# The first layer of a two-layer graph network as seven products of quadrants with 129-column halves, the second norm's operand in one buffer, and the residual in the second step

## The chip, the cores and the metric

The kernel runs on one core of one Trainium2 chip. The metric is device time in microseconds (us) of one execution of the program; the median of three runs before the change is 2427.76 us (2426.85 to 2429.27). Below, PE is the matrix engine (TensorE) and PEld its loading of the stationary operand, DVE is VectorE, ACT is ScalarE, POOL is GpSimd and SP is SyncE, which issues the DMAs. L137 is line 137 of the kernel, where every matmul is recorded; L35 is the helper that records nearly every operation of the other engines, so that these are told apart by their tiles.

## The reference

Two layers of graph attention over x of shape (64, 256, 512) in float32, with one 256x256 adjacency matrix for the whole batch. Each layer takes a layer norm and a relu of x and adds its output to x.

```python
# layer 0
h = jnp.maximum(_layernorm(x), 0.0)
H = jnp.einsum('bnf,fo->bno', h, W)              # 512 -> 256
e = H @ a[0] + swapaxes(H @ a[1], 1, 2)          # 256 x 256 per batch
e = leaky_relu(e, 0.2) - 1e9 * (1 - adj)
out = softmax(e, -1) @ H
x = x + concatenate([out, H], -1)
# layer 1: 8 heads of 64
h = jnp.maximum(_layernorm(x), 0.0)
q, k, v = (split_heads(h @ W.T + b) for each of q, k, v)
attn = softmax(where(adj == 0, -inf, q @ k.T / 8), -1)
x = x + merge_heads(attn @ v) @ Wo.T + bo
```

## The kernel before, in words

The 64 batches are taken in 32 groups `g` of two batches `b` (512 tokens, four row tiles of 128). There is no hardware loop: everything is unrolled, and generators that stand for stages are advanced by hand. Group `g` is in its attention (`scores`, `mask_pairs`, `fold`, `weigh`, `outputs`) while group `g+1` is in `project` (q, k, v), group `g+2` in `first_layer` and group `g+3` in `first_norm`. One period is one group; it has two steps, b = 0 and b = 1, each with a string (`steps`) of letters that says in which order the stages advance: S the scores, m masking of a pair of heads, n a piece of the first norm, s a piece of `first_layer`, u a product of `project`, o a product of `outputs`, f a piece of `fold` (the row sums of the attention), r half of `residual`, v `value_differences`. The step (g=0, b=0) has a string of its own. At the start of a step, `weigh` emits the products p·v of the step before (tile `pr`), and the scores (`sc`) follow.

What fixes the order on each engine: all matmuls and transposes of PE are pinned in the order in which they are written (`in_order`). On the other engines `not_sooner` pins an operation behind the one written last on its engine; operations without it are placed by the tile framework's scheduler. SP's DMA issues are pinned as well, and a DMA waits in SP's queue until its data is there.

PSUM: matmul results take one of five banks in turn (`mm`, tag `turn`), so that a product can start only when the bank that was used five allocations ago has been read; three more banks are held for `project` and `outputs`. The pr banks of a step are read by DVE into `oT0` and `oT1` (with `r`, the reciprocals of the row sums); the scores take eight banks, `sc_0` to `sc_7`, two in alternation, and `sc_3` comes round to the bank that `oT0` frees.

The first norm: DVE takes the statistics of `x`, POOL a power and a factor of them (`factor`), ACT normalizes into `xn` (two buffers), DVE transposes 32x32 blocks into `xt`, a DMA writes them out (`passed`), four DMAs fetch them (`moved`), and ACT copies them with a relu into the operand: `hT0` for the first layer, one 128x4x256 tile for each batch, and `hT1` for the second, one 128x4x512 tile for each group.

The first layer: 258 columns, which are two score columns (`W` times the two vectors of `a`) and behind them the 256 of `W`. For each of four row tiles, four matmuls of 128 rows by 258 columns over 512 features add up in one bank `ph`, ACT copies it into `H`, and POOL adds H to the right half of x. Then `rows` (a DVE transpose of the score columns), a DMA through DRAM to `own`, four ACT additions into `e`, leaky relu of `e` on DVE (`scalar_tensor_tensor`, twice, both inputs in SBUF), exp on ACT, masking on DVE and the products `po`.

The projections q, k and v and the outputs are done already as seven products of quadrants instead of eight (a scheme of Winograd's: `operand_sums` makes s1 = a21+a22, s2 = s1−a11, s3 = a11−a21 and s4 = a12−s2, and overwrites a21 with s3; `weight_sums` does the like for the weights; `seven` says which operand meets which weight). Their results are assembled with a product kept in SBUF (tag `kept`, three buffers) and one or two products that add up in a bank.

The residual: `residual(g+1)` adds the rows `b_out` of the output bias to x of group g+1, four POOL operations of 128x512. It is written in the first step of each period.

Of the kernel before, what the change touches and what calls it, by code (L numbers as in the profile page):

```python
# [57 lines left out]
def bounded(  # L58
# [50 lines left out]
    def mm(name):  # L109
        return psum.tile([P, 512], F32, tag="turn", name=name, bufs=5)  # L110
# [25 lines left out]
    def matmul(*args, **kwargs):  # L136
        in_order(nc.tensor.matmul(*args, **kwargs))  # L137
# [28 lines left out]

    w0_sb = const.tile([P, HP, F1 + 2], F32, name="w0_sb")
    nc.sync.dma_start(w0_sb[:, :, 2:], w0.rearrange("(c p) o -> p c o", p=P))
    adj_i = att.tile([P, NT, N], I32, tag="kept", name="adj_i", bufs=3)
    nc.sync.dma_start(adj_i, adj.rearrange("(t p) k -> p t k", p=P))  # L170

# [79 lines left out]
    square_ones = big.tile([P, P], F32, tag="o_sums", name="square_ones", bufs=1)  # L251
    gpsimd.memset(square_ones, 1.0)

    def weight_sums(name):
        w = w_sb[name]
        not_sooner(vector, "tensor_sub", w[:, :, T3, :], w[:, :, W22, :], w[:, :, W12, :])
        vector.tensor_sub(w[:, :, T1, :], w[:, :, W12, :], w[:, :, W11, :])
        vector.tensor_sub(w[:, :, T2, :], w[:, :, W22, :], w[:, :, T1, :])
        vector.tensor_sub(w[:, :, T4, :], w[:, :, W21, :], w[:, :, T2, :])

    def last_bias():

# [230 lines left out]

    def operand_sums(engine, quads, sums):
        a11, a12, a21, a22 = quads
        not_sooner(engine, "tensor_add", sums[:, 0], a21, a22)
        engine.tensor_sub(sums[:, 1], sums[:, 0], a11)

        not_sooner(engine, "tensor_sub", a21, a11, a21)
        engine.tensor_sub(sums[:, 2], a12, sums[:, 1])  # L500

    def seven(quads, sums):

        a11, a12, s3, a22 = quads
        s1, s2, s4 = (sums[:, i] for i in range(3))
        return {
            1: (a11, W11), 2: (a12, W21), 3: (s4, W22), 4: (a22, T4),  # L510
            5: (s1, T1), 6: (s2, T2), 7: (s3, T3),
        }
# [5 lines left out]
    def first_norm(g):  # L518

        xt = {}  # L520
        mv = small.tile([P, GT, 2], F32, tag="mv", name=f"mv0_{g}", bufs=4)
        factors, norm, turn, fetch, put = norm_T(xt, mv, f"0_{g}", g == 0)
        for b in range(GB):
            for t in range(NT):
                xt[b * NT + t] = xs[g, b][:, t, :]
                stats(mv, xt, b * NT + t, f"0_{g}")
            factors(b)
            yield
            norm(b)
            yield  # L530
            turn(b)
            if g == 1:
                fetch(b)
            yield
            if g <= 1:

                other = g == 0 and b == 1
                pool, tag, bufs = (att, "moved", 2) if other else (big, "hT0", 1)
                hT0[g, b] = pool.tile([P, HP, N], F32, tag=tag, name=f"hT0_{g}_{b}", bufs=bufs)
                put(b, hT0[g, b])  # L540
                if g == 1:
                    yield
        if g <= 1:
            return
        for b in range(GB):
            fetch(b, b == 1 or g == 2)
        yield
        for b in range(GB):
            hT0[g, b] = big.tile([P, HP, N], F32, tag="hT0", name=f"hT0_{g}_{b}", bufs=1)
            put(b, hT0[g, b])  # L550
            yield


    H = const.tile([P, GT, F1 + 3], F32, name="H")
    gpsimd.memset(H[:, :, F1 + 2 :], 1.0)

    def first_layer(g):

        xt = [xs[g, b][:, t, :] for b in range(GB) for t in range(NT)]
        for r in range(GT):  # L560
            b, t = divmod(r, NT)
            ph = mm(f"ph_{g}_{r}")[:, : F1 + 2]
            for c in range(HP):
                matmul(
                    ph, hT0[g, b][:, c, t * P : (t + 1) * P], w0_sb[:, c, :],
                    start=(c == 0), stop=(c == HP - 1),
                )
            scalar.copy(H[:, r, : F1 + 2], ph)
            if g < 2:
                gpsimd.tensor_add(xt[r][:, F1:], H[:, r, 2 : F1 + 2], xt[r][:, F1:])  # L570
            else:
                not_sooner(
                    gpsimd, "tensor_add", xt[r][:, F1:], H[:, r, 2 : F1 + 2], xt[r][:, F1:]
                )
            if r < GT - 1:
                yield

        pT = {}
        if g:

            rows = small.tile([P, GT, 8], F32, tag="rows", name=f"rows_{g}", bufs=2)
            not_sooner(vector, "transpose", rows.rearrange("p t c -> p (t c)"), H[:, :, 0:8])
            line = dram.tile([P // 8, S], F32, tag="line", name=f"line_{g}")
            not_sooner(sync, "dma_start", line, rows.rearrange("p t c -> p (t c)")[::8, :])
            own = att.tile([P, P // S, GT, S], F32, tag="r", name=f"own_{g}", bufs=1)
            not_sooner(
                sync, "dma_start", own.rearrange("p k t j -> p (k t j)"),
                line.rearrange("(o k) j -> o (k j)", o=1).to_broadcast([P, TOK]),
            )
            own = own.rearrange("p k t j -> p t k j")  # L590
            yield
        else:
            yield
            pn = mm(f"pn_{g}")
            for t in range(GT):
                transpose(pn[:, t * P : (t + 1) * P], H[:, t, 0:1].to_broadcast([P, P]), ident)
            own = pn.rearrange("p (t k j) -> p t k j", t=GT, j=S)
# [25 lines left out]
        for r in range(GT):  # L623
# [20 lines left out]
                    turn(0)  # L644
                    fetch(0)
            yield
        hT = big.tile([P, HP, TOK], F32, tag="hT1", name=f"hT1_{g}")
        sums = big.tile([P, 3, 2, N], F32, tag="sums", name=f"sums_{g}", bufs=1)
        quads = [
            hT[:, 2 * c : 2 * c + 2, r * N : (r + 1) * N] for r in range(2) for c in range(2)  # L650
        ]
# [165 lines left out]
    def fold(g, b, p):  # L817
# [4 lines left out]
            return  # L822
        compact = small.tile([P, NQ, N // S], F32, tag="compact", name=f"compact_{g}_{b}", bufs=2)
        row_sums[g, b] = compact
        pool, tag = (att, "e") if b == 0 else (big, "hT0")
        rows = []

        def put(quad):
# [2 lines left out]
            not_sooner(sync, "dma_start", rows[quad], p[:, heads, 0, :])  # L831

        def fetch(quad):
            parts = pool.tile([P, P // S, N], F32, tag=tag, name=f"parts_{g}_{b}_{quad}", bufs=1)
# [35 lines left out]
    def weigh(g, b, p):  # L870
# [36 lines left out]
        places.append(v_tag)  # L907
        quads = [oTs[c][:, :, r * P : (r + 1) * P] for r in range(2) for c in range(2)]
        sums = big.tile([P, 3, 2, P], F32, tag="o_sums", name=f"o_sums_{g}_{b}", bufs=1)
        operand_sums(vector, quads, sums)  # L910
        operands["o", g, b] = seven(quads, sums)

# [49 lines left out]
    def run(part):  # L962
        for _ in part:
            pass
# [36 lines left out]
    order = "n - - - - - nss s s ss ss s s n n sn - s n".split()  # L1001
    for i, parts in enumerate(order, 2):
        next(products)
        if i in (2, 8):
            weight_sums("kv"[i // 7])
        for part in parts:
            if part != "-":
                next(norms if part == "n" else pieces, None)
        next(verdict, None)
        if i in (6, 9, 11):  # L1010
            next(bias)
        if i == 15:
            run(residual(0))
    run(verdict)


    steps = ("Smmnfuuuumonmruofssfnuufrssouvfnofunonosuo", "Ssmmfusmusmfuososfuosfsusuonufsonufouunous")
    waiting, late, folds = None, iter(()), iter(())
    for g in range(NG):
        products = project(g + 1) if g + 1 < NG else iter(())  # L1020
        pieces = first_layer(g + 2) if g + 2 < NG else iter(())
        for b, parts in enumerate(steps):
            if g == b == 0:

                parts = "Smmnnuuuumnnfmrufssfnufrssuufvnunfunsu"
            elif g == NG - 1:
                parts = "Smmoomoomooo"
            if waiting is not None:
                weigh(*waiting)
                late = outputs(*waiting[:2])  # L1030
            i, count = -1, sum(part not in "frv" for part in parts)
            additions = residual(g + 1) if b == 0 and g + 1 < NG else iter(())
            for part in parts:
                i += part not in "frv"
                if part == "u":
# [23 lines left out]
                if "v" not in parts and i == (count * 3 // 4, 6)[b] and g < NG - 1:  # L1059
                    value_differences(g, b)  # L1060
                if i == count // 2:
                    if g == b == 0:
                        weight_sums("o")
                    if g == max(NG - 2, 0) and b == 1:
                        conclude()
                    if "r" not in parts:
                        run(additions)
                    if g + 3 < NG:
                        load(g + 3, b)
        run(products)  # L1070
# [374 lines left out]
```

## Time and profile before

| What | us |
|---|---|
| median of three runs | 2427.76 |
| the profiled execution | 2427.79 |
| its span in the trace | 2426.1 |
| PE busy | 2398.9 (99%) |
| PEld busy | 2003.0 (83%) |
| DVE busy | 1659.5 (68%) |
| POOL busy | 1294.2 (53%) |
| ACT busy | 1012.5 (42%) |
| first-layer matmuls `ph` (1024 records) | 235.6 |
| the period of one group | 74.07 |
| its first step and its second | 37.92 and 36.15 |

A float32 matmul shows as two MATMUL records on PE and two LDWEIGHTS records on PEld. A record's duration is the time from its start to its end, and the next one starts before that end; what PE pays for a record is the distance between starts. The profile runs on the core's own clock, from the start of the program, and the granted TensorE clock is 0.999 of full speed over the execution.

The period that the prediction follows in detail begins at 391.98 us of the trace, with the scores of a first step; its second step begins at 429.90.

### The profile page before, as it was taken

Reading aid. Unit: us, or ns where it says so; the run is one execution under the profiler, and the core shown is the slowest. Engines: PE = TensorE matmul, PEld = TensorE weight load, DVE = VectorE, ACT = ScalarE, POOL = GpSimd, SP = SyncE. Lnnn points to the kernel's source line nnn. Section 1 sums busy time; section 2 is a strip of 40 time slices with the busy share of each in tenths; the row PEclk is TensorE's granted clock in tenths of the full one; section 3 lists DMA queues with packets and bytes.
Section 4 is the critical chain, followed back from the end, with each engine's and each line's share of the span. In section 5 each row is a group of like instructions: output and inputs, shape, how many; then the busy total and the mean of one; then the engine's idle time right before and its main releaser. Section 6 shows DMA issues by size and latency. Waiting matters only on the chain.

```text
span 2426.1 us, 41175 instructions
## 1 busy us (share of the span) xinstructions
PE 2398.9 (99%) x15052; PEld 2003.0 (83%) x15052; DVE 1659.5 (68%) x3252; ACT 1012.5 (42%) x2017; POOL 1294.2 (53%) x1214
## 2 busy tenths in 40 slices
PE   8899999999999999999999999999999999999998
PEld 7778888888888888888888888888888888888886
DVE  7676766776766767667766667676677676676656
ACT  5543443444444434434434444344344344343431
POOL 2545656545556446565455564465654555645551
PEclk9999999999999999999999999999999999999999
DMA  6345445545455454455454454544553544545331
GB/s 195 100 123 156 135 144 153 159 124 158 138 153 156 136 152 136 143 152 153 130 161 135 153 156 136 152 136 143 152 163 120 161 135 153 157 132 156 114 108 45
DMA packets 272033, 343.64 MB, mean 142 GB/s; under 512 B 25425, under 2 KB 217169, under 8 KB 271825
## 3 DMA queue, kind: packets, MB, share of 16 engines
q1 hardware_dynamic: 271824, 340.95, 46.0%
q8 instruction: 120, 1.97, 0.3%
q14 instruction: 89, 0.72, 0.1%
HBM read 177.22 MB, written 163.64 MB: 140 GB/s over the span
## 4 chain that ended last, share of the span: by engine, by line
PE 97%; DMA 1%; DVE 1%; ACT 1%; issue 0%; SPq 0%; POOL 0%; DVEq 0%; POOLq 0%; ACTq 0%
PE py L137 16%; PE pq L137 16%; PE pk L137 16%; PE pv L137 16%; PE sc L137 10%; PE pr L137 9%; PE ph L137 9%; PE po L137 5%; DMA moved<-passed 0%; PE pt L140 0%; SPq L35 0%; DMA passed<-xt 0%; PE total L137 0%; DMA x<-in_x_dram 0%; PE gram_q L137 0%
## 5 line engine op out<-in xcount | busy, mean ns | idle before, releaser
L35 POOL TENSOR_TENSOR p<-p 128x512 f32<-128x512 f32 x248 | 404.7, 1648 | 512.7 <-DVE p L35 511.4
L35 DVE TENSOR_TENSOR p<-p,maskT 128x1024 f32<-128x1024 f32 x254 | 328.7, 1314 | 1.2 <-ACT p L35 1.2
L35 ACT ACTIVATE xn<-x,factor 128x512 f32<-128x512 f32 x256 | 194.5, 807 | 298.3 <-POOL factor L35 298.2
L35 POOL TENSOR_TENSOR parts<-parts 128x512 f32<-128x512 f32 x248 | 247.5, 998 | 119.3 <-DMA parts<-rows 104.1
L35 ACT ACTIVATE p<-sc 128x512 f32<-128x512 f32 x512 | 257.8, 627 | 111.9 <-PE sc L137 95.0
L35 DVE TENSOR_TENSOR x<-py,x 128x256 f32<-128x256 f32 x448 | 185.5, 414 | 146.0 <-PE py L137 140.4
L137 PE MATMUL py<-wo_sb,oT 128*128 128x256 f32 x1024 | 262.4, 379 | 0.6 <-DVE oT L35 0.6
L35 POOL TENSOR_TENSOR factor<-factor,rexp 128x2 f32<-128x2 f32 x128 | 120.1, 938 | 264.7 <-DVE factor L35 263.9
L137 PE MATMUL sc<-q,k 64*128 64x256 f32 x2048 | 252.5, 389 | 0.4 <-ACT p L35 0.4
L137 PEld LDWEIGHTS sc<-q,k 64*128 64x128 f32 x2048 | 211.0, 186 | 42.4 <-issue 26.3
L137 PE MATMUL pk<-hT,wk_sb 128*128 128x256 f32 x1024 | 244.7, 382 | 0.0
L137 PE MATMUL pr<-p,v 128*32 128x256 f32 x4096 | 235.8, 382 | 5.5 <-POOL v L35 5.5
L137 PE MATMUL pq<-hT,wq_sb 128*128 128x256 f32 x1024 | 239.9, 382 | 0.0
L137 PE MATMUL ph<-w_sb,hT 128*128 128x258 f32 x1024 | 235.6, 382 | 2.2 <-ACT hT L35 2.2
L137 PE MATMUL pv<-wv_sb,hT 128*128 128x256 f32 x1024 | 237.0, 379 | 0.4 <-ACT kept_v L35 0.4
L137 PEld LDWEIGHTS ph<-w_sb,hT 128*128 128x128 f32 x1024 | 194.2, 190 | 32.9 <-ACT hT L35 3.2
L137 PEld LDWEIGHTS pk<-hT,wk_sb 128*128 128x128 f32 x1024 | 192.1, 190 | 35.3 <-issue 10.4
L137 PEld LDWEIGHTS pq<-hT,wq_sb 128*128 128x128 f32 x1024 | 191.8, 190 | 35.3 <-issue 9.9
L137 PEld LDWEIGHTS py<-wo_sb,oT 128*128 128x128 f32 x1024 | 194.1, 190 | 28.2 <-DVE oT L35 1.1
L137 PEld LDWEIGHTS pv<-wv_sb,hT 128*128 128x128 f32 x1024 | 194.4, 190 | 27.2 <-ACT kept_v L35 0.8
L137 PEld LDWEIGHTS pr<-p,v 128*32 128x32 f32 x4096 | 127.0, 110 | 104.6 <-issue 21.8
L137 PE MATMUL py<-wo_sb,o_sums 128*128 128x256 f32 x768 | 197.5, 379 | 0.5 <-DVE x L35 0.5
(131 smaller groups left out, 3784.9 us busy)
## 6 DMA issues: line engine op xcount, KB each, us to landing
passed<-xt SPq DMA_DIRECT2D x124, 512.0 KB, 2.7
moved<-passed SPq DMA_DIRECT2D x496, 128.0 KB, 3.1
rows<-p SPq DMA_DIRECT2D x124, 512.0 KB, 3.4
parts<-rows SPq DMA_DIRECT2D x496, 128.0 KB, 3.0
x<-in_x_dram SPq DMA_DIRECT2D x64, 512.0 KB, 4.9
out_dram<-x SPq DMA_DIRECT2D x62, 512.0 KB, 3.7
own<-line SPq DMA_DIRECT2D x31, 256.0 KB, 3.1
wq_sb<-in_L_gnn_Wq_dram SPq DMA_DIRECT2D x2, 512.0 KB, 8.5
```

The costliest lines, as they stand in the source:

```text
L35: instruction = getattr(self.engine, operation)(*args, **kwargs)
L137: in_order(nc.tensor.matmul(*args, **kwargs))
```

## The change

- The first layer of groups 2 to 31 is done as seven products of quadrants (`first_products`). The quadrants of the operand are 256 features x 256 tokens (one batch), those of the weight 256 features x 129 columns. Each product is 2 token tiles x 2 feature tiles = 4 matmuls of 129 columns, 28 for a group instead of 16 of 258. ACT keeps three products in SBUF, DVE makes three quadrants of `H` from a bank and a kept product, ACT copies the fourth. Groups 0 and 1 are done as before.
- `operand_sums` on POOL makes s1 (in tag `r`), s2 and s4 (in tag `xn`) for the first layer of each of these groups; `first_weight_sums` makes the sums of the weights once, at the start, on POOL.
- `weight_sums("o")` moves from DVE in the step (g=0, b=0) to POOL in the setup.
- `hT1` has one buffer instead of two; `hT0` has two instead of one, for which both copies into `hT0` now come in one piece of `first_norm`. The row sums' `parts` of b = 1, which take turns in that tag, have two buffers as well.
- POOL adds H to x once for each batch (128x512) instead of once for each row tile (128x256); `rows` is made after the fourth of these products instead of after the last matmul.
- `residual(g+1)` is written in the second step of a period, right behind the scores, instead of in the first.
- The strings of the steps are rewritten.

```diff
+    def first_weight_sums():
+        w11, w12, w21, w22 = (
+            w0_sb[:, 2 * c : 2 * c + 2, h * FH : (h + 1) * FH] for c in range(2) for h in range(2)
+        )
+        t2, t3, t4 = (w0_more[:, i] for i in range(3))
+        not_sooner(gpsimd, "tensor_sub", t3, w22, w12)
+        not_sooner(gpsimd, "tensor_sub", w12, w12, w11)
+        not_sooner(gpsimd, "tensor_sub", t2, w22, w12)
+        not_sooner(gpsimd, "tensor_sub", t4, w21, t2)
...
         for b in range(GB):
-            hT0[g, b] = big.tile([P, HP, N], F32, tag="hT0", name=f"hT0_{g}_{b}", bufs=1)
+            hT0[g, b] = big.tile([P, HP, N], F32, tag="hT0", name=f"hT0_{g}_{b}")
             put(b, hT0[g, b])
-            yield
+            if b == 0:
+                yield
+        quads = [hT0[g, b][:, 2 * c : 2 * c + 2, :] for b in range(GB) for c in range(2)]
+        sums = [
+            att.tile([P, 2, N], F32, tag=tag, name=f"sums0_{g}_{tag}", bufs=bufs)
+            for tag, bufs in (("r", 1), ("xn", 2), ("xn", 2))
+        ]
+        operand_sums(gpsimd, quads, sums)
+        operands["first", g] = {i: form[0] for i, form in seven(quads, sums).items()}
+        yield
...
+    def first_products(g):
+        ops = operands.pop(("first", g))
+        forms = {
+            1: w0_sb[:, :2, :FH], 2: w0_sb[:, 2:, :FH], 3: w0_sb[:, 2:, FH:], 5: w0_sb[:, :2, FH:],
+            6: w0_more[:, 0], 7: w0_more[:, 1], 4: w0_more[:, 2],
+        }
...
+        def product(out, i, start):
+            a = ops[i]
+            for t in range(NT):
+                for c in range(2):
+                    matmul(
+                        out[:, t, :], a[:, c, t * P : (t + 1) * P], forms[i][:, c, :], start=start and t == c == 0,
+                        stop=t == c == 1, skip_group_check=True,
+                    )
...
+        first = bank(1)
+        product(first, 1, True)
+        p1 = kept(first, 0)
+        yield
+        second = bank(2)
+        product(second, 2, True)
+        vector.tensor_add(part(0, 0), second, p1)
+        yield
+        product(first, 6, False)
+        p16 = kept(first, 1)
+        yield
+        second = bank(7)
+        product(second, 7, True)
+        p7 = kept(second, 2)
+        yield
+        product(first, 5, False)
+        vector.tensor_add(part(1, 1), first, p7)
+        yield
+        product(second, 4, False)
+        vector.tensor_add(part(1, 0), second, p16)
+        owns[g] = score_rows(g)
+        residual_from(1)
+        yield
+        product(first, 3, False)
+        scalar.copy(part(0, 1), first)
+        residual_from(0)
...
-        hT = big.tile([P, HP, TOK], F32, tag="hT1", name=f"hT1_{g}")
+        hT = big.tile([P, HP, TOK], F32, tag="hT1", name=f"hT1_{g}", bufs=1)
...
+        if i == 7:
+            weight_sums("o", gpsimd)
+        if i == 9:
+            first_weight_sums()
...
-    steps = ("Smmnfuuuumonmruofssfnuufrssouvfnofunonosuo", "Ssmmfusmusmfuososfuosfsusuonufsonufouunous")
+    steps = ("Smmnfuuuumonmnuofuusssosfsfssuvnofunofnosuo", "Srrsmmfusmusmfuososfuosfsuuonufounfouunsous")
...
-                parts = "Smmnnuuuumnnfmrufssfnufrssuufvnunfunsu"
+                parts = "Smmnnuuuumnnfmnufuuvssssfsfssunfunfnsuu"
...
-            additions = residual(g + 1) if b == 0 and g + 1 < NG else iter(())
+            additions = residual(g + 1) if b == 1 and g + 1 < NG else iter(())
...
-                    if g == b == 0:
-                        weight_sums("o")
```

More of the change, by code (lines that the diff above doesn't have):

```diff
@@ L168, in bounded @@
     nc.sync.dma_start(w0_sb[:, :, 2:], w0.rearrange("(c p) o -> p c o", p=P))
+    FH = F1 // 2 + 1
+    w0_more = const.tile([P, 3, 2, FH], F32, name="w0_more")
     adj_i = att.tile([P, NT, N], I32, tag="kept", name="adj_i", bufs=3)
@@ L252, in bounded, with weight_sums @@
     gpsimd.memset(square_ones, 1.0)
-    def weight_sums(name):
+    def weight_sums(name, engine=vector):
         w = w_sb[name]
[L256 to L259, printed above, removed]
+        not_sooner(engine, "tensor_sub", w[:, :, T3, :], w[:, :, W22, :], w[:, :, W12, :])
+        engine.tensor_sub(w[:, :, T1, :], w[:, :, W12, :], w[:, :, W11, :])
+        engine.tensor_sub(w[:, :, T2, :], w[:, :, W22, :], w[:, :, T1, :])
+        engine.tensor_sub(w[:, :, T4, :], w[:, :, W21, :], w[:, :, T2, :])
+    def first_weight_sums():
[7 more added lines that the diff above has]
+        not_sooner(gpsimd, "tensor_sub", t4, w21, t2)
     def last_bias():
@@ L495, in operand_sums @@
         a11, a12, a21, a22 = quads
-        not_sooner(engine, "tensor_add", sums[:, 0], a21, a22)
-        engine.tensor_sub(sums[:, 1], sums[:, 0], a11)
+        s1, s2, s4 = sums
+        not_sooner(engine, "tensor_add", s1, a21, a22)
+        engine.tensor_sub(s2, s1, a11)
         not_sooner(engine, "tensor_sub", a21, a11, a21)
-        engine.tensor_sub(sums[:, 2], a12, sums[:, 1])
+        engine.tensor_sub(s4, a12, s2)
     def seven(quads, sums):
         a11, a12, s3, a22 = quads
-        s1, s2, s4 = (sums[:, i] for i in range(3))
+        s1, s2, s4 = sums
         return {
@@ L535, in first_norm @@
             if g <= 1:
-                other = g == 0 and b == 1
-                pool, tag, bufs = (att, "moved", 2) if other else (big, "hT0", 1)
-                hT0[g, b] = pool.tile([P, HP, N], F32, tag=tag, name=f"hT0_{g}_{b}", bufs=bufs)
+                hT0[g, b] = big.tile([P, HP, N], F32, tag="hT0", name=f"hT0_{g}_{b}")
                 put(b, hT0[g, b])
@@ L548, in first_norm @@
         for b in range(GB):
-            hT0[g, b] = big.tile([P, HP, N], F32, tag="hT0", name=f"hT0_{g}_{b}", bufs=1)
+            hT0[g, b] = big.tile([P, HP, N], F32, tag="hT0", name=f"hT0_{g}_{b}")
             put(b, hT0[g, b])
-            yield
+            if b == 0:
[5 more added lines that the diff above has]
+        ]
@@ L554, in bounded, with score_rows @@
+        operand_sums(gpsimd, quads, sums)
+        operands["first", g] = {i: form[0] for i, form in seven(quads, sums).items()}
+        yield
     H = const.tile([P, GT, F1 + 3], F32, name="H")
     gpsimd.memset(H[:, :, F1 + 2 :], 1.0)
+    owns = {}
+    def score_rows(g):
+        rows = small.tile([P, GT, 8], F32, tag="rows", name=f"rows_{g}", bufs=2)
+        not_sooner(vector, "transpose", rows.rearrange("p t c -> p (t c)"), H[:, :, 0:8])
+        line = dram.tile([P // 8, S], F32, tag="line", name=f"line_{g}")
+        not_sooner(sync, "dma_start", line, rows.rearrange("p t c -> p (t c)")[::8, :])
+        own = att.tile([P, P // S, GT, S], F32, tag="r", name=f"own_{g}", bufs=1)
+        not_sooner(
+            sync, "dma_start", own.rearrange("p k t j -> p (k t j)"),
+            line.rearrange("(o k) j -> o (k j)", o=1).to_broadcast([P, TOK]),
+        )
+        return own.rearrange("p k t j -> p t k j")
@@ new lines, in first_products, with bank, part, kept @@
+    def first_products(g):
[4 more added lines that the diff above has]
+        }
+        def bank(name):
+            return mm(f"ph{name}_{g}")[:, : NT * FH].rearrange("p (t o) -> p t o", t=NT)
+        def product(out, i, start):
[5 more added lines that the diff above has]
+                        stop=t == c == 1, skip_group_check=True,
+                    )
+        def part(b, half):
+            return H[:, b * NT : (b + 1) * NT, half * FH : (half + 1) * FH]
+        def kept(out, i):
+            s = att.tile([P, 2, N], F32, tag="kept", name=f"kept{i}_h_{g}", bufs=3)
+            s = s.rearrange("p t n -> p (t n)")[:, : NT * FH].rearrange("p (t o) -> p t o", t=NT)
+            scalar.copy(s, out)
+            return s
+        def residual_from(b):
+            xt = xs[g, b][:, :, F1:]
+            not_sooner(gpsimd, "tensor_add", xt, H[:, b * NT : (b + 1) * NT, 2 : F1 + 2], xt)
+        first = bank(1)
[24 more added lines that the diff above has]
+        residual_from(0)
@@ L557, in first_layer @@
     def first_layer(g):
         xt = [xs[g, b][:, t, :] for b in range(GB) for t in range(NT)]
-        for r in range(GT):
+        if g > 1:
+            yield from first_products(g)
+        for r in range(GT if g <= 1 else 0):
             b, t = divmod(r, NT)
@@ L568, in first_layer @@
             scalar.copy(H[:, r, : F1 + 2], ph)
[L569 to L574, printed above, removed]
+            gpsimd.tensor_add(xt[r][:, F1:], H[:, r, 2 : F1 + 2], xt[r][:, F1:])
             if r < GT - 1:
@@ L578, in first_layer @@
         pT = {}
[L579 to L590, printed above, removed]
+        if g > 1:
+            own = owns.pop(g)
+            yield
+        elif g:
+            own = score_rows(g)
             yield
@@ L646, in first_layer @@
             yield
-        hT = big.tile([P, HP, TOK], F32, tag="hT1", name=f"hT1_{g}")
+        hT = big.tile([P, HP, TOK], F32, tag="hT1", name=f"hT1_{g}", bufs=1)
         sums = big.tile([P, 3, 2, N], F32, tag="sums", name=f"sums_{g}", bufs=1)
+        sums = [sums[:, i] for i in range(3)]
         quads = [
@@ L824, in fold @@
         row_sums[g, b] = compact
-        pool, tag = (att, "e") if b == 0 else (big, "hT0")
+        pool, tag, bufs = (att, "e", 1) if b == 0 else (big, "hT0", 2)
         rows = []
@@ L833, in fetch @@
         def fetch(quad):
-            parts = pool.tile([P, P // S, N], F32, tag=tag, name=f"parts_{g}_{b}_{quad}", bufs=1)
+            parts = pool.tile([P, P // S, N], F32, tag=tag, name=f"parts_{g}_{b}_{quad}", bufs=bufs)
             for j in range(QH):
@@ L909, in weigh @@
         sums = big.tile([P, 3, 2, P], F32, tag="o_sums", name=f"o_sums_{g}_{b}", bufs=1)
+        sums = [sums[:, i] for i in range(3)]
         operand_sums(vector, quads, sums)
@@ L1061, in bounded @@
                 if i == count // 2:
-                    if g == b == 0:
-                        weight_sums("o")
                     if g == max(NG - 2, 0) and b == 1:
                         conclude()
-                    if "r" not in parts:
-                        run(additions)
                     if g + 3 < NG:
```

## The prediction

> **What bounds the kernel now.** I read the page's totals first, then the chain of waits, then busy time by stretches, then one period of each engine.
>
> ```profile
> PE 2398.9 (99%) x15052; PEld 2003.0 (83%) x15052; DVE 1659.5 (68%) x3252; ACT 1012.5 (42%) x2017; POOL 1294.2 (53%) x1214
> ...
> PE 97%; DMA 1%; DVE 1%; ACT 1%; issue 0%; SPq 0%; POOL 0%; DVEq 0%; POOLq 0%; ACTq 0%
> ```
>
> PE is busy for 99% of the span and makes 97% of the chain that ends last. Stretches of 370 us (five periods; the columns are PE, PEld, DVE, ACT and POOL) show where the other 1% is:
>
> ```profile
> 100.00:470.00 370.00, 362.75 (x2276) 301.51 (x2274) 255.38 (x492) 154.92 (x306) 207.57 (x191) 1.00 0.47 142
> 470.00:840.00 370.00, 370.00 (x2320) 310.02 (x2320) 253.52 (x501) 156.44 (x311) 202.32 (x190) 1.00 0.49 146
> 1950.00:2320.00 370.00, 370.00 (x2321) 309.79 (x2319) 250.68 (x486) 153.32 (x306) 203.07 (x188) 1.00 0.47 142
> ```
>
> From 470 to 2320 us PE never stands still. So a microsecond less of matmuls is a microsecond less of time, as long as no other engine is late; and any lateness costs in full. Times below without "of the trace" count from the start of the first step at 391.98 us; its second step begins at 37.92.
>
> **Part 1, the products.** A timeline row gives the matmuls of two row tiles, and the view of one tile a shape that the new matmuls resemble:
>
> ```profile
> 413.23 3.65 PE L137 MATMUL ph<-w_sb,hT 128*128 128x258 f32 x16
> 416.72 1.02 PE L137 MATMUL py<-wo_sb,o_sums 128*128 128x256 f32 x4
> ```
>
> ```profile
> L137 PEld LDWEIGHTS gram_q<-wq_sb x32: 186/192/192, 21.3 to 24.7; 128*128 128x128 f32 x32
> L137 PE MATMUL gram_q<-wq_sb x32: 275/275/289, 21.3 to 24.8; 128*128 128x128 f32 x32
> ```
>
> From 413.23 to 416.72 are 3.49 us for 16 records, 0.217 each between single starts: a group's 32 pay 6.94. The 129 columns have no row; the nearest is gram_q with 128: 32 records start within 3.5 us, so 31 steps of about 0.112. Loads of 0.190 thus overlap each other, which is what the halved matmuls need. New: 28 matmuls, 56 records x 0.112 = 6.27. Gain 0.67 us a group, over 30 groups 20 us. Bounds: with the 0.109 of the kernel's transposes, 6.10, gain 0.84 (25 us); if the products' double waits and handovers each lose 0.1 at this quick pace, four times, gain 0.3 (8 us). Full loss of overlap is a rival.
>
> [...]
>
> **Part 2, the sums on POOL.** Four additions of 128x512 at 1.27 (`x<-x,b_out`: 160.4 us / 128 = 1.25 with overlap) are 5.1 us a group. They lie at about 14.8 to 19.9, where the residual's first half goes out. s2 is due by the third product (19.5), s3 by the fifth (21.2), s4 by the last (23.9): slack 2.1, 1.5 and 4. Cost 0; were POOL 2.1 us late, PE would pay the excess.
>
> **Part 3, handovers.** ACT's four copies (0.373) become three of 2x129 columns and one into H (about 0.6 each, by `hT` copies of 128x512), in ACT's idle time. DVE gets three additions at 0.69 (`q<-pq,kept`) in idle stretches from 14.94 to 23.15. The tightest two: the kept first product is copied by 19.24, its bank is loaded for again at 19.45, covered by the second product's 0.9 us; the addition into H's fourth quadrant ends at 23.73 and its bank is wanted at 23.89. Cost 0, bound 0.5 a group (15 us) if both are 0.25 later than their slack.
>
> **Part 4, the buffers.** With one `hT1`, ACT's copies for the next group wait for PE's last reader, at about 67.3 instead of 64.16. ACT idles 5.29 us from 65.30 now, until the copy of v at 70.58, so two copies (1.14) fit. `hT0` and `parts` only gain a buffer; the moved `passed`, `moved` and `own` DMAs (2.7, 3.1 and 3.1 to landing) keep over 1 us before their readers. Cost 0; without ACT's gap it would be 1.1 a period.
>
> **Part 5, the residual.** This decides, I think. Four POOL operations leave 15.8 to 18.3 and 23.1 to 25.6 and stand behind the second `parts` sum, which ended at 31.2. POOL's row says that it was idle there, and DVE's what runs meanwhile:
>
> ```profile
> 421.10 2.08 POOL L35 TENSOR_TENSOR parts<-parts 128x512 f32<-128x512 f32 x2
> 434.74 3.41 POOL L35 TENSOR_TENSOR p<-p 128x512 f32<-128x512 f32 x2 [11.55 <-DVE p L35]
> ```
>
> ```profile
> 426.42 0.42 DVE L35 TENSOR_TENSOR x<-py,x 128x256 f32<-128x256 f32 x1 [0.55 <-PE py L137]
> 426.87 1.49 DVE L35 SCALAR_TENSOR_TENSOR e<-e 128x512 f32<-128x512 f32 x2
> 428.27 0.70 DVE L35 STREAM_TRANSPOSE r<-compact 128x512 f32<-128x512 f32 x1
> 429.08 0.69 DVE L35 TENSOR_TENSOR oT<-pr,r 128x512 f32<-128x512 f32 x1
> ```
>
> POOL idles 11.55 us up to 434.74. The residual fills 31.2 (or 31.7, as the second `parts` are fetched up to 0.5 later) to 36.2 or 36.7. In it fall DVE's two leaky relus (`e<-e`), with two SBUF inputs. Such operations are held while POOL works:
>
> ```profile
> L35 DVE TENSOR_TENSOR wo_sb<-wo_sb x4: 1156/1642/1644, 105.6 to 110.1; 128x512 f32<-128x512 f32 x4
> L35 DVE SCALAR_TENSOR_TENSOR e<-e x64: 649/692/693, 22.4 to 2279.6; 128x512 f32<-128x512 f32 x64
> L35 DVE TENSOR_TENSOR o_sums<-oT,oT x64: 424/426/1507, 135.7 to 2415.0; 128x256 f32<-128x256 f32 x64
> ```
>
> The min, median and max show it: the same 128x512 subtraction takes 0.69 in wq_sb, with POOL idle, and 1.64 here, beside POOL; `o_sums` 0.43 or 1.51. `e<-e` is at 0.69 in all 64, and in all of them POOL is idle. That it is held too is unshown, so its cost has two ends: 0, and about 1.8 (both relus held for nearly an operation each, 2 x 0.95, less 0.08 of slack).
>
> The Trainium skill, "SBUF — State Buffer", on who interferes with whom, says that a DVE instruction with two SBUF inputs contends with a POOL instruction that reads SBUF, the later one waiting for the other's end. By it the hold is certain; by the rows it is likely.
>
> Is DVE late then? The last `py` product ends at 34.44, in the new order 33.74 (0.7 earlier). DVE's queue behind it is: addition 0.42, reciprocal 0.17, two `xt` transposes (0.62 and 0.59; before, they ran at 31.5 to 33.1), the relus, the r transpose 0.63, then oT0. Scores bank `sc_3` needs oT0's bank, 4.71 us after that product's end (34.44 to 39.15). Without a hold, with 0.04 after the product and 0.15 behind oT0: 0.04+0.42+0.17+0.62+0.59+0.61+0.61+0.63+0.1+0.69+0.15 = 4.63; before, oT0 ended at 37.80, 1.35 early. So the transposes eat the slack, and 0.08 is left. With a hold the first relu, asked for at 35.46, starts at 36.2 to 36.7: 0.74 to 1.24 late; PE stalls 0.66 to 1.16. I take 0.95, near the middle. Late next would be the masking of p, with ACT's exponentials behind the stall; the second step is long enough for them.
>
> **Part 6, the start.** Two sets of weight sums go to POOL, 4 x 1.27 and 4 x 0.65 (`parts` of 256 and `x<-H,x` are 0.69 to 0.73), in its idle stretches at 47.7 to 59.7 and 62 to 76.6 of the trace: 0. DVE loses four at 1.52 in the first step, where PE waits 5.5 us for POOL's `v` (before it stand the `parts`): with v first that goes, but the kept copy of product 1 stands behind the next group's operand copies and costs some 3.4. Net −1.8, range −5 to 0.
>
> **Sum.** 30 x (−0.67) = −20.1; 29 x 0.95 = 27.6; start −1.8. Together +5.7 on the profiled execution's 2427.8 (span 2426.1 and 1.7 around it; the median is the same to 0.03): 2433.5.
>
> **Rivals.**
> - A: the products' gain stays, because the relus aren't held or their hold finds slack that I missed. For: `e<-e` has never shown it, my slack is a sum of eleven rows, and POOL may reach the last addition 0.5 earlier. Against: the `wo_sb` row. −20.1−1.8 and some remaining stall of 0 to 0.2 (0 to 6): 2406 to 2412.
> - B, the worse side: both relus are held, or `xt` transposes also wait for their write-out, stall 1.5 to 1.8 a period: −22 + 29 x 1.65 = +26: 2454. It decides from 0.67 a period on, where the gain is used up; for it: POOL starts another addition as soon as the first relu is done, if it is 1 us later than I lay it.
> - C: the narrow matmuls don't overlap their loads: 28 x 2 x 0.190 = 10.64 against 6.94, +3.7 x 30 = 111, 2537. Against: gram_q's pace with the same 0.192 loads.
> - D: handovers of part 3 miss by 0.25 each on top of A's gain: −22+15, 2421; on top of the forecast, 2448.
>
> **How the numbers follow.** Chances: forecast 0.42 (own range 2425 to 2440, from its stall's ends), A 0.28, B 0.14, D 0.13, C 0.03. Predicted 2433. The range, A's lower end and B's upper, 2406 to 2452, leaves out B's end and C. A measurement of this kernel tells about 0.2% from no change: 2422.9 to 2432.6. A and D's better half lie below (0.28 + 0.07), B, C, D's other half and most of the forecast above; of the forecast 0.14 falls inside, with 0.02 of the rest: faster 0.34, same 0.16, slower 0.50.
>
> **What would show it.** Starts of `ph` records 0.112 apart (C: 0.19). `e<-e` at 1.4 to 1.9 for one of two, with `x<-x,b_out` over it (A: 0.69). PE idle about 0.95 in front of `sc` once a period, released by DVE's oT; in stretches of 370 us PE busy about 365 instead of 370. A wait before the third or last `ph` product would be D's. If PE has no idle time and the period is 73.4, A is right and part 5 wrong.

## The result, and the profile after

The changed kernel takes 2440.69 us (median of five runs, 2438.24 to 2444.41) against 2429.01 (2426.85 to 2429.67) for the kernel before, run beside it: a ratio of 1.0052, 95% interval 1.0037 to 1.0067. It is slower by half a per cent. The forecast was 2433 us, a loss of 5.7 us, inside a range (2406 to 2452) that holds gains too; the medians show a loss of 11.7. The mechanism of the steady state is the one that was thought likeliest; most of what the forecast lacks lies in the start, whose sign it had wrong.

The page of the changed kernel, engine totals and the chain that ended last (shares by engine, then by line and tile):

```profile
PE 2396.2 (98%) x15772; PEld 2014.3 (83%) x15772; DVE 1746.7 (72%) x3338; ACT 1023.1 (42%) x2017; POOL 1437.7 (59%) x1282
...
PE 92%; DVE 4%; DMA 2%; issue 1%; ACT 1%; SPq 1%; POOL 0%; ACTq 0%; DVEq 0%; POOLq 0%
PE py L137 16%; PE pv L137 15%; PE pq L137 15%; PE pk L137 15%; PE sc L137 10%; PE ph L137 8%; PE pr L137 7%; PE po L137 4%; DVE oT L35 1%; DVE e L35 1%; DVE xt L35 1%; SPq L35 1%; DMA own<-line 0%; DVE r L35 0%; DMA passed<-xt 0%
```

PE's part of the chain falls from 97% to 92%, and DVE's `oT`, `e` and `xt` are in it now: DVE ends waits that did not exist. The busy time by stretches of 370 us (PE, PEld, DVE, ACT, POOL) says that this happens in every period:

```profile
100.00:470.00 370.00, 357.78 (x2301) 302.23 (x2300) 260.48 (x499) 153.17 (x300) 225.62 (x198) 0.98 0.46 140
470.00:840.00 370.00, 368.23 (x2436) 310.26 (x2435) 271.17 (x513) 158.35 (x310) 224.78 (x200) 1.00 0.47 146
1950.00:2320.00 370.00, 367.80 (x2435) 309.87 (x2434) 265.81 (x504) 157.10 (x308) 226.25 (x198) 1.00 0.46 141
```

In the second and third row PE is idle for 1.8 and 2.2 us in five periods, in the three rows between them for up to 2.9; before it was 0 in all of them. The idle time understates the loss: scores that trickle out one bank at a time overlap their neighbours less and count as busy. The scores' row of before, then the one of the changed kernel:

```profile
L137 PE MATMUL sc<-q,k 64*128 64x256 f32 x2048 | 252.5, 389 | 0.4 <-ACT p L35 0.4
L137 PE MATMUL sc<-q,k 64*128 64x256 f32 x2048 | 268.7, 391 | 20.1 <-DVE oT L35 19.7
```

As many records, hardly longer each (391 ns for 389), are busy for 16.2 us more. The waits of PE name the place (waited for: us in total, times, longest; the wait for `xn` is the kernel's very beginning, and was 8.7 before):

```profile
PE sc L137 <- DVE oT L35: 19.7, 30, 5.7
PE pt L140 <- ACT xn L35: 8.1, 1, 8.1
PE ph L137 <- POOL sums_xn L35: 3.3, 1, 3.3
```

Once in a period the scores wait for `oT`, which frees their bank. One ordinary period (its second step starts at 511.15) shows why, DVE's timeline first, then POOL's:

```profile
508.16 1.24 DVE L35 STREAM_TRANSPOSE xt<-xn 128x512 f32<-128x512 f32 x2
509.33 2.23 DVE L35 SCALAR_TENSOR_TENSOR e<-e 128x512 f32<-128x512 f32 x2
511.48 0.70 DVE L35 STREAM_TRANSPOSE r<-compact 128x512 f32<-128x512 f32 x1
512.28 1.29 DVE L35 TENSOR_TENSOR oT<-pr,r 128x512 f32<-128x512 f32 x2
```

```profile
503.38 2.08 POOL L35 TENSOR_TENSOR parts<-parts 128x512 f32<-128x512 f32 x2
505.42 4.98 POOL L35 TENSOR_TENSOR x<-x,b_out 128x512 f32<-128x512 f32 x4
517.58 3.41 POOL L35 TENSOR_TENSOR p<-p 128x512 f32<-128x512 f32 x2 [7.18 <-DVE p L35]
```

The two relus take 2.23 instead of 1.49 in the period shown of before, because the first, asked for at 509.33, ends only at 510.95, 0.55 us after POOL's residual (505.42 to 510.40) does. `oT0` is done at 512.97, and the fourth score bank starts at 513.03, 1.88 us after the step's start; without the wait, in the first experiment below, it starts 1.18 after it. Over the whole run the relus are no longer all alike:

```profile
L35 DVE SCALAR_TENSOR_TENSOR e<-e x64: 648/1303/1774, 23.9 to 2293.9; 128x512 f32<-128x512 f32 x64
```

Minimum, median and maximum were 649, 692 and 693 ns before. The products themselves are as quick as forecast. In the same period (PE):

```profile
496.12 1.06 PE L137 MATMUL ph<-w_sb,sums_r 128*128 128x129 f32 x8
497.02 1.06 PE L137 MATMUL ph<-w_more,hT 128*128 128x129 f32 x8
497.91 1.08 PE L137 MATMUL ph<-w_sb,sums_xn 128*128 128x129 f32 x8
```

Eight records start within 0.89 to 0.90 us, 0.112 each.

The starts of the scores divide the run into steps; differences after less before, in us, of the two profiled executions:

| Part of the run | before | after | difference |
|---|---|---|---|
| up to the first scores | 89.92 | 91.69 | +1.8 |
| step (g=0, b=0) | 44.88 | 41.58 | −3.3 |
| step (0, 1) | 34.42 | 42.92 | +8.5 |
| step (1, 0) | 38.48 | 37.23 | −1.3 |
| 28 first steps, g = 2 to 29 | 37.92 (one 38.16) | 37.22 each | −19.8 |
| 29 second steps, g = 1 to 29 | 36.15 each | 36.96 to 38.03 | +28.3 |
| the rest | | | 0.0 |

In sum +14.2, for the profiled executions' 2442.23 less 2427.79 = 14.4. The products give 0.70 us in every period and the residual takes 0.98 on average: in 18 of the 29 periods 0.82, in the others up to 1.88, where POOL's `parts` came later. The rest is the start, +5.7, and in it the step (0, 1). SP's second fetch of the first group's row sums, before and after, and PE's scores after:

```profile
122.40 1.73 SPq L35 DMA_DIRECT2D parts<-rows  x4
126.93 1.74 SPq L35 DMA_DIRECT2D parts<-rows  x4
140.55 5.14 PE L137 MATMUL sc<-q,k 64*128 64x256 f32 x22 [5.73 <-DVE oT L35]
```

### The profile page after: what moved, and what is told of

Its sections match the earlier page's. It is cut to its first block, busy times and chain, and to the rows that moved or that the text cites. A ratio compares the mean times of both kernels' runs of the same rounds, so it can differ in the third digit from the quotient of the medians.

```text
span 2440.6 us, 42947 instructions
## 1 busy us (share of the span) xinstructions
PE 2396.2 (98%) x15772; PEld 2014.3 (83%) x15772; DVE 1746.7 (72%) x3338; ACT 1023.1 (42%) x2017; POOL 1437.7 (59%) x1282
## 4 chain that ended last, share of the span: by engine, by line
PE 92%; DVE 4%; DMA 2%; issue 1%; ACT 1%; SPq 1%; POOL 0%; ACTq 0%; DVEq 0%; POOLq 0%
PE py L137 16%; PE pv L137 15%; PE pq L137 15%; PE pk L137 15%; PE sc L137 10%; PE ph L137 8%; PE pr L137 7%; PE po L137 4%; DVE oT L35 1%; DVE e L35 1%; DVE xt L35 1%; SPq L35 1%; DMA own<-line 0%; DVE r L35 0%; DMA passed<-xt 0%
## 5 line engine op out<-in xcount | busy, mean ns | idle before, releaser
L35 POOL TENSOR_TENSOR p<-p 128x512 f32<-128x512 f32 x248 | 395.9, 1610 | 347.4 <-DVE p L35 347.4
L35 DVE TENSOR_TENSOR p<-p,maskT 128x1024 f32<-128x1024 f32 x254 | 338.5, 1352 | 1.2 <-ACT p L35 1.2
L137 PE MATMUL sc<-q,k 64*128 64x256 f32 x2048 | 268.7, 391 | 20.1 <-DVE oT L35 19.7
L137 PE MATMUL pq<-sums,wq_sb 128*128 128x256 f32 x768 | 181.5, 379 | 0.9 <-POOL hT L35 0.9
L137 PE MATMUL pv<-wv_sb,sums 128*128 128x256 f32 x768 | 181.5, 379 | 0.0
```

The lines of the kernel that those rows point to most:

```text
L35: instruction = getattr(self.engine, operation)(*args, **kwargs)
```

## The experiments

**The residual elsewhere.** POOL has an idle gap behind the third fold piece of the second step, over which DVE has no operation with two SBUF inputs. All the residual goes there, or half of it.

```diff
-    "Srrsmmfusmusmfuososfuosfsuuonufounfouunsous"
+    "Ssmmfusmusmfuososfrruosfsuuonufounfouunsous"   # e1_late
+    "Srsmmfusmusmfuososfruosfsuuonufounfouunsous"   # e2_half
```

> The residual of the next group stays in the second step, but stands on POOL behind the third fold piece instead of right behind the scores: into POOL's idle 5.4 us at 59.1 to 64.5 of a period, where DVE has no operation with two SBUF inputs. Theory H (DVE's leaky relus are held by POOL's residual): e<-e is back at 0.65 to 0.69 in all periods, PE waits 0.1 us or less in front of the second step's fourth score bank, the second step takes 36.15 to 36.25 us, the period 73.4, the time falls by 27 to 29 us against the changed kernel's 2440.7, to 2411 to 2415: faster than before the change by 0.6%. Rival T (the two xt transposes that moved behind the reciprocal make oT0 late, whatever POOL does): e<-e is at 0.69 as well, but PE's wait of about 0.8 stays in each period, 2438 to 2441. Rival R (the residual only moves its hold to other DVE operations): the second step stays above 36.8.

> Two of the residual's four POOL operations stay behind the scores, the other two go behind the third fold piece. Theory H: the two end at about 34.8 of a period and the first relu is asked for at 35.4, so nothing is held in most periods; in the quarter of the periods in which the parts came 0.5 to 1.2 us late, one relu is held by up to 0.5. Time 0 to 5 us above the version with all four moved, 2411 to 2420. A rival by which the loss goes with the amount of POOL work in that stretch, not with its overlap with the relus, gives half of the loss: 2425 to 2429. Rival T: 2438 to 2441.

All of it late: 2415.26 us (2411.95 to 2416.05), ratio to before 0.9938 (0.9925 to 0.9952). Half of it: 2413.25 (2412.63 to 2414.78), 0.9934 (0.992 to 0.9947). DVE and POOL with all of it late, in the same period (second step from 507.83):

```profile
504.85 1.24 DVE L35 STREAM_TRANSPOSE xt<-xn 128x512 f32<-128x512 f32 x2
506.01 1.25 DVE L35 SCALAR_TENSOR_TENSOR e<-e 128x512 f32<-128x512 f32 x2
```

```profile
500.06 2.08 POOL L35 TENSOR_TENSOR parts<-parts 128x512 f32<-128x512 f32 x2
513.29 3.41 POOL L35 TENSOR_TENSOR p<-p 128x512 f32<-128x512 f32 x2 [11.15 <-DVE p L35]
...
526.04 2.08 POOL L35 TENSOR_TENSOR parts<-parts 128x512 f32<-128x512 f32 x2
528.08 4.95 POOL L35 TENSOR_TENSOR x<-x,b_out 128x512 f32<-128x512 f32 x4
```

With POOL idle up to 513.29 the relus take 1.25 for both. Every second step is back at 36.15 and every first one stays at 37.22: the 28.3 us are gone to 0.0, although the transposes stand where the change put them, and PE does not stand still in this stretch:

```profile
470.00:840.00 370.00, 370.00 (x2479) 313.62 (x2469) 265.81 (x518) 159.39 (x313) 226.56 (x203) 1.00 0.48 149
```

That is theory H; T and R fall. Half of the residual, ending 1.4 us before the first relu, costs nothing either, so it is the overlap that costs and not the amount of work in the stretch.

**Is it the reading?** The late residual, and in its old place work of no use to the result: eight additions that read two inputs, or sixteen memsets that only write. The letter `w` stands twice where the change has its two `r`.

```diff
...
+                elif part == "w":
+                    for _ in range(4 if g + 1 < NG else 0):
+                        not_sooner(gpsimd, "tensor_add", scratch, b_out[:, : D // 2], b_out[:, D // 2 :])  # e7_reads
+                    for _ in range(8 if g + 1 < NG else 0):
+                        not_sooner(gpsimd, "memset", scratch, 0.0)                                          # e8_writes
```

> The late residual, and besides eight POOL additions of 128x256 (both inputs rows of b_out, the result into a scratch tile that nothing reads) where the changed kernel has its residual, behind the scores of the second step; some 8 x 0.65 = 5.2 us. Theory: any POOL additions there hold the relus; each relu is held to the end of an operation of half the length, so by 0 to 0.65 instead of 0 to 1.26: relus at 0.7 to 1.4, PE's wait in a period 0.2 to 1.1, 2418 to 2440. If the hold were a matter of the residual's own data (x just read or written by others), the relus are at 0.69 and the time is the late residual's 2413 to 2416.

> As the run with the eight additions, but sixteen memsets of 128x256 of the same scratch tile in their place, which write and read nothing; by the page's memset rows (128x128 0.204, 128x32 0.124) some 16 x 0.31 = 4.9 us. If POOL's reading of SBUF is what holds DVE's second input, the relus stay at 0.65 to 0.69 and the time is that of the late residual, 2413 to 2416. If any POOL operation holds them, or the issue of so many, the relus are at 0.8 to 1.2 and the time is 2417 to 2435.

With additions 2428.23 (2424.87 to 2429.43), with memsets 2414.13 (2410.62 to 2414.84). The additions, POOL's row and DVE's:

```profile
503.13 7.11 POOL L35 TENSOR_TENSOR scratch<-b_out 128x256 f32<-128x256 f32 x8
```

```profile
507.05 1.80 DVE L35 SCALAR_TENSOR_TENSOR e<-e 128x512 f32<-128x512 f32 x2
```

The memsets:

```profile
502.22 5.84 POOL L35 MEMSET scratch<- 128x256 f32 x16
```

```profile
506.15 1.25 DVE L35 SCALAR_TENSOR_TENSOR e<-e 128x512 f32<-128x512 f32 x2
```

Both POOL rows lie over the relus (7.11 us to 510.24, 5.84 to 508.06). Beside additions the two take 1.80; beside memsets 1.25, as with POOL idle. So POOL operations that read SBUF, whatever data, hold a DVE operation with two SBUF inputs, and those that only write do not (a memset is shorter, 0.31 us, but no relu took over 0.70 beside them); shorter additions hold it for less (the second steps are 13.6 us longer in sum, not 28.3). The Trainium skill, "SBUF — State Buffer", section "Who interferes with whom", says this in both halves: a POOL instruction that reads contends, one that only writes does not. These two runs agree with it. The hold works both ways: the additions' slowest takes 1.24 where the median takes 0.73.

**The transposes.** First the last norm piece was put ahead of the last fold piece in the first step, then in addition the `passed` DMA behind `own` on SP; the residual stays where the change put it.

```diff
-    "Smmnfuuuumonmnuofuusssosfsfssuvnofunofnosuo"
+    "Smmnfuuuumonmnuofuusssosfsfssuvnofunonfosuo"   # e3_xt
...
-            sync.dma_start(passed[b], xt.rearrange("p j c t n -> p j (c t n)"))
+            if b == 0 and name.startswith("0_") and int(name[2:]) > 3:          # e11_xt_own, besides
+                not_sooner(sync, "dma_start", passed[b], xt.rearrange("p j c t n -> p j (c t n)"))
+            else:
+                sync.dma_start(passed[b], xt.rearrange("p j c t n -> p j (c t n)"))
```

> The residual stays where the change put it; the turn piece of the first norm goes ahead of the fold piece in the first step's string, so that DVE's two xt transposes run before the parts transposes, as before the change. Theory H: the first relu is asked for about 1.1 us earlier, at 34.3, and is held to the end of POOL's second or third operation (34.8 or 36.0), the second one for another; one or both relus at 1.1 to 1.8, PE's wait in a period 0.2 to 0.8 instead of 0.82 to 1.4: 2424 to 2438. Rival T: the wait is gone, 2411 to 2415.

> The changed kernel with its residual where it is, the turn piece ahead of the fold piece as in the earlier try, and the passed DMA of that turn pinned on SP behind own, which it had overtaken there. Theory: the relus are asked for at 34.3 instead of 35.4 and still held (one or both at 1.1 to 1.8), but the 1.1 us of DVE's transposes are back as slack: PE's wait 0 to 0.5 in a period instead of 0.82 to 1.9, 2413 to 2430. Were slack not what decides, the wait would follow the hold, 0.8 and more: 2437 to 2445.

The first took 2502.83 us (2499.51 to 2503.67), far off both expectations, and tells nothing of the question, for it moved something else. SP's queue in it:

```profile
506.31 0.53 SPq L35 DMA_DIRECT2D line<-rows  x1
511.82 0.34 SPq L35 DMA_DIRECT2D passed<-xt  x1
512.27 0.37 SPq L35 DMA_DIRECT2D own<-line  x1
```

`own`, the operand of the additions into `e`, now stands behind `passed`, which waits for the transposes. It goes out 6.0 us after `line` instead of 2.9 as in the changed kernel; the relus come after the scores have begun, ACT's exponentials of the scores stand behind those of `e`, and PE waits 55.1 us in 29 periods for ACT.

With `own` first, 2437.29 us (2436.14 to 2437.65). This misses the 2413 to 2430 that was expected, and lies in the range set for the case that the wait follows the hold and not the slack (2437 to 2445). DVE and POOL in one period (second step from 511.35):

```profile
508.72 2.88 DVE L35 SCALAR_TENSOR_TENSOR e<-e 128x512 f32<-128x512 f32 x2 [0.27 <-ACT e L35]
511.52 0.70 DVE L35 STREAM_TRANSPOSE r<-compact 128x512 f32<-128x512 f32 x1
```

```profile
505.62 5.43 POOL L35 TENSOR_TENSOR x<-x,b_out 128x512 f32<-128x512 f32 x4
```

The relus are asked for earlier and held longer, 2.88 for both: the second ends at 511.60, again 0.55 us behind POOL's last addition (511.05). Second steps in most periods are 36.80 instead of 36.97. With the residual in this place, the late transposes are 0.16 of the usual loss of 0.82; the end of the residual sets the rest.

**The residual alone.** The kernel before, with its residual moved; the last fold piece goes behind the last norm piece, so that the residual still follows the second `parts` sum on POOL.

```diff
-    steps = ("Smmnfuuuumonmruofssfnuufrssouvfnofunonosuo", "Ssmmfusmusmfuososfuosfsusuonufsonufouunous")
+    steps = ("Smmnfuuuumonmuofssfnuufssouvfnofunonfosuo", "Srrsmmfusmusmfuososfuosfsusuonufsonufouunous")
...
-            additions = residual(g + 1) if b == 0 and g + 1 < NG else iter(())
+            additions = residual(g + 1) if b == 1 and g + 1 < NG else iter(())
```

> The kernel before, with its residual alone moved behind the scores of the second step (and the last fold piece behind the last norm piece, which keeps the residual behind the second parts sum on POOL); first layer, buffers and xt transposes as before. Theory: POOL's four operations run at 31.2 to 36.3, the relus asked for at 34.9 are held by up to 1.3 each, but oT0 had 1.35 us of slack here, because the xt transposes run before: PE's wait 0 to 0.5 in a period, 2429 to 2443. If the residual's place alone costs what it costs in the changed kernel, 0.8 to 1.4 a period: 2453 to 2470.

2432.4 us (2431.28 to 2435.51), ratio to before 1.0016 (1.0007 to 1.0026). In the period whose second step begins at 508.90:

```profile
505.87 2.34 DVE L35 SCALAR_TENSOR_TENSOR e<-e 128x512 f32<-128x512 f32 x2
508.13 0.70 DVE L35 STREAM_TRANSPOSE r<-compact 128x512 f32<-128x512 f32 x1
```

The hold is much the same (2.34 for two instead of 2.23), and the steps stay at 37.92 and 36.15: both sums over the run change by under 1 us. The small loss lies in the start (PE waits 8.7 instead of 5.5 us for POOL's `v`). So the hold costs nothing where the chain is 1.35 early. In the changed kernel the residual ends 0.74 us before the second step's start instead of 1.84, since the `parts` ahead of it on POOL are later, and the same bank is wanted just as soon after that start.

**The start.** Three runs on the version with the late residual, each containing the one before: fold pieces earlier in the string of the step (0, 0); the power operation of group 3's factors pinned on POOL behind what is written ahead of it; two additions into H of group 2 pinned on DVE behind the first `parts` transposes.

```diff
-                parts = "Smmnnuuuumnnfmnufuuvssssfsfssunfunfnsuu"
+                parts = "Smmnnuuuumnnfmnufuufvssssfsssunfunfnsuu"      # e5_late_start
...
-            if name == "0_0":
+            if name in ("0_0", "0_3"):                                  # e6_start_pin, besides
                 not_sooner(gpsimd, "tensor_tensor", rstd, ve, rexp, op=ALU.pow)
...
+        if g == 2:                                                      # e10_start_dve, besides
+            not_sooner(vector, "tensor_add", part(1, 1), first, p7)
...
+        if g == 2:
+            not_sooner(vector, "tensor_add", part(1, 0), second, p16)
...
```

> As the version with the residual behind the third fold piece, and in the string of the step (g=0, b=0) the third and fourth fold pieces earlier: the first row sums' additions ahead of the value differences, their transposes ahead of the score rows. Theory: the 8.5 us that the step after it lost comes from the row sums' second fetch, which SP issues at 126.9 instead of 122.4 of the trace because POOL's and DVE's work on the first row sums stands behind the new sums and additions; issued by 123, oT0 comes 4 to 5 us earlier, and the time is 3 to 6 us below the version without this. Rival: another chain is as late (own, x, v) and the time is the same within 1 us.

> As the version with the earlier fold pieces in the step (g=0, b=0), and the power operation of the first norm's factors of group 3 pinned on POOL behind what is written ahead of it, so that it no longer stands between the two sums of the first parts: there it waits for DVE's statistics from 120.5 to 126.0 of the trace, and the second sum with it. Theory: the second sum runs at 120.5, the parts transposes at about 121.5, SP issues the second fetch at 122.5 instead of 128.4, oT0 comes 4 to 5 us earlier, and PE's 4.6 us wait at the scores of the step after shrinks to 0 to 1.5: 2409 to 2412, that is 3 to 5 us below the versions with the late residual. Rival: `own` or the first norm is late next, and less than 1 us comes of it.

> As the version with the pinned power operation, and DVE's two additions into H of group 2 that use the fifth and the fourth product pinned behind the first parts transposes, which the run before left behind the score rows and the statistics (at 126.9 of the trace, with the parts sums done at 121.8). Theory: transposes at 122 to 123, second fetch issued at 123 to 124, oT0 3.5 to 4.5 us earlier, PE's 4.0 us wait at the scores falls to 0 to 0.7: 2407 to 2410, the fastest of all. Rival: own, whose DMA stands behind the fetch, or the additions into H late next: 2410 to 2413.

The first gave 2414.59 us (2413.14 to 2416.12), no change: POOL's second sum of the first `parts` still waited behind the factor. The second gave 2411.49 (2410.89 to 2415.01), inside the expected 2409 to 2412, but not as the theory had it: PE's wait at the scores fell only from 4.6 to 4.0 us, not to 1.5 or less. POOL's sums were done in time, but DVE's transposes of them still stood behind the score rows and the statistics, and step (0, 1) lost 7.5 us as before. With both pinned it is 2405.76 us (2404.77 to 2408.33), a little under the 2407 to 2410 expected, and step (0, 1) is 34.42 again, without its wait and its slow clock. The theory was right; the order had to be undone on both engines. This version is the fastest: ratio to before 0.9905 (0.9889 to 0.9922).

## Why the prediction was right, point by point

The side and the mechanism of the steady state came as forecast. The number is less good: 2440.7 lies just above the forecast's own 2425 to 2440, at double its loss, and the range of 2406 to 2452 is wide.

- *Products, 0.67 us a group.* Right: 0.70 in each period, −19.8 over the 28 that can be compared plainly, against −20.1 for 30. The row of `gram_q` gave the pace (0.112). Rival C, loads that don't overlap, did not come.
- *Sums, handovers, buffers at nothing (parts 2 to 4).* Right in the steady state: with the residual out of the way PE is busy for 370.00 of 370.00 us again, so rival D's misses did not come. They were not priced in the first group, see below.
- *The residual, 0.95 us a period.* Right in place, mechanism and size: 0.82 in the usual period, 0.98 on average, 28.3 us in sum for 27.6. That the sum fits so closely is partly luck, since 11 late periods make up for the others. PE was busy for 367.1 to 368.2 of 370 us instead of the 365 given as a sign, as scores that trickle count as busy. That the relus are held, which no row of before showed, is shown by moving the work, and by additions against memsets. The sum of eleven rows was good: with the hold gone and the transposes late PE just does not wait. Rival B's stall of 1.5 to 1.8 was reached once (1.88); in ten other periods, where the `parts` were late too, the loss was 0.9 to 1.4. Rival A's time, 2406 to 2412, is what the kernel takes, nearly, when the residual is elsewhere (2413 and 2415). Two readings of the working are off: the `wq_sb` rows at 0.69 do not have POOL idle, for three of the four run beside small `factor` operations (128x2), so they show the unheld length but not an idle POOL; and the gain is used up from 0.69 a period on by the products alone, or 0.76 with the start's −1.8, not from 0.67.
- *The start, −1.8 (range −5 to 0).* Wrong, and the one term that was mis-sized: it measured +5.7. The 5.5 us wait for `v` did go, as said. But idle time was only looked for under the weight sums. The second fetch of the first group's row sums was not followed: it stood behind the new sums on POOL, a factor that waits for DVE, and H's additions on DVE, and SP issued it at 126.93 instead of 122.40. `oT0` began at 139.80 instead of 133.28; part of that is the residual's hold, for with the residual late the step (0, 1) lost 7.4 us instead of 8.5. The late residual, the earlier fold pieces and the two pins together brought it to 0.0. Of the wait that the forecast put at 3.4, the size came (3.29) and not the cause: it was not for the kept copy of the first product, which ACT made at 111.01, but for the operand s2 of the next one, whose sums POOL began at 112.49. And that PE runs slowly behind such a wait was left out.

The 1.8 us up to the first scores were not tried by themselves. PE's second group of matmuls starts at 11.53 us of the trace, after 1.47 of waiting for DVE's `prod`, and before at 10.47 without a wait; DVE had waited for the load of `w_sb` until 10.53 instead of 9.46. Why the load came later stays open. In the experiments on the changed kernel this stretch took 2.3 to 5.3 us more than in the kernel before; what goes beyond some 2 us is in the last section.

## What to carry to other kernels

Before moving work to an idle stretch of POOL, list what DVE does in that stretch with two inputs in SBUF, and let each of those end no earlier than shortly after the POOL operation that it meets (0.55 us here for a relu of 128x512); then ask how early the chain behind them is. Idle time on one engine is not free if what fills it holds another engine. And lay out the first period by itself: a steady state with slack says nothing of a start in which each queue stands behind another.

## What the runs showed of the hardware that was not expected

A wait of PE can cost more than its length. PE in the first group of the changed kernel, and the granted clock there (first number after POOL's):

```profile
115.15 2.09 PE L137 MATMUL ph<-w_more,sums_xn 128*128 128x129 f32 x8 [3.29 <-POOL sums_xn L35]
117.03 1.93 PE L137 MATMUL ph<-w_more,hT 128*128 128x129 f32 x8
118.75 1.93 PE L137 MATMUL ph<-w_sb,sums_r 128*128 128x129 f32 x8
120.47 1.47 PE L137 MATMUL ph<-w_more,hT 128*128 128x129 f32 x8
121.78 1.06 PE L137 MATMUL ph<-w_sb,sums_xn 128*128 128x129 f32 x8
```

```profile
112.00:115.00 3.00, 0.00 (x0) 0.00 (x0) 0.40 (x1) 1.16 (x3) 2.43 (x2) 0.91 0.70 180
115.00:118.00 3.00, 2.85 (x13) 2.85 (x14) 0.00 (x0) 0.38 (x1) 3.00 (x4) 0.50 0.51 169
118.00:121.00 3.00, 3.00 (x16) 3.00 (x16) 0.21 (x1) 0.38 (x1) 1.99 (x2) 0.50 0.00 0
121.00:124.00 3.00, 3.00 (x22) 2.85 (x22) 2.17 (x6) 0.38 (x1) 0.00 (x0) 0.95 0.00 0
```

After 3.29 us of waiting the clock is at 0.50 from about 114.5 (0.91 on average in the first row) to 121.3 (0.95 in the last): eight records take 1.72 to 1.88 instead of 0.90, some 3 us more in all, as much again as the wait. The Trainium skill, "TensorE: Matmul & The Clock Gate", section "What's actually happening", has the clock halve after an idle window of about 3.4 us whose phase runs freely. These runs don't bear out the length: here the clock fell some 2.6 us after PE's last record, in a wait of 3.29, and the measurement decides.

At the kernel's very start PE waits for `e` in every run on the changed kernel, and the length of the wait does not tell what the clock does. It stayed at 1.00 behind 3.13 us in the changed kernel and behind 2.90 in the first try of the transposes, where the first scores began at 91.7 and 92.2. In four runs (2.89 to 3.34 us) it was at 0.50 for 3.4 us (0.86 on average from 69 to 81 us of the trace), and the first scores began at 93.5 to 93.9. In the late-residual run (3.11), the fastest one (3.38) and two more it was at 0.50 for 6.8 us, from about 71 to 78 (0.72 on average), and they began at 94.6 to 95.2. That is how one stretch of unchanged work took up to some 3 us more in one execution than in another. A phase that runs freely would account for it; no run here sets the phase.
